# Moving the start of a background job inside one pair of a four-layer convolution kernel

## The chip, the cores and the metric

The kernel runs on one core of a Trainium2 chip, in one launch. The metric is the device time of that launch in microseconds (us); the time before is the median of three runs.

## What is computed

The input x has the shape 1024 x 16 x 16 x 16 (batch, height, width, channels), in float32. Four residual layers follow one another, each behind a group norm with 8 groups of 2 channels (mean and variance over height, width and the 2 channels of each sample):

```python
x = x + L0(gn(x))   # a tensor-train matrix on the 4096 values of a sample: cores of ranks 1, 16, 16, 1
x = x + L1(gn(x))   # a cellular automaton step: two depthwise 3x3 convolutions, 48 -> 128 -> 16 dense, an alive mask
x = x + L2(gn(x))   # a 3x3 convolution, 16 -> 16 channels
x = x + L3(gn(x))   # as L1, with other weights
```

The change lies in layer 0. What matters of the rest is that layer 1 needs the mean and the reciprocal root of the variance of layer 0's output, for each sample and group.

## The kernel before

**Halves and tiles.** The batch is cut in two halves of 512 samples. Two large SBUF tiles of 128 partitions x 32 x 512 floats, `XN[0]` and `XN[1]` (`xn` in the profile), hold activations. Layer 0 is done as 13 *pairs* (the rows of the table `OUTER`; `j` in the code, counted from 0). A pair multiplies combinations of input blocks by combinations of weight blocks. Pair j keeps its input in `XN[j % 2]`; the other large tile is being filled for pair j + 1.

**The foreground of a pair.** A pair has four *units* (u, by q from 0 to 3), and a unit has seven products (k from 0 to 6), each in two halves. So a pair has 4 x 7 x 2 = 56 *steps*, 14 to a unit; step 14 is the first of the second unit. A step issues eight matmuls (L1586). Around them, by the number of the step in its unit, stand: at 1 the store of the unit before (with one negated copy, L1553, and accumulating DMAs to `xf` on the queue of GpSimd, L1560); at 2, 4, 6, 12 and 13 a `mix` on VectorE, which makes the weights that a product needs from sums of blocks (L1508 and L1510): the ones at 12 and 13 (`s2`, `s5`) are for the next unit, whose first two products read them; at 5 and 9 a `build` of the next unit's weights, which is 32 small matmuls (L1478) and four copies on ScalarE (L1483); at 7 and 11 the loads for the unit after the next (`gq`; on GpSimd's queue at L1464 for pair 11, on SyncE's at L1459 for pair 12). After each second half a `gather` takes the product from PSUM: for the products 2, 3 and 6 in one VectorE addition of 128 x 1024 (L1622), for 4 and 5 in one of 128 x 512 (L1632), for 0 and 1 on ScalarE (L1628, L1630). In the first unit of a pair, ten additions on VectorE (L1220) also make the combined inputs of the pair.

**The order.** Every engine runs its instructions in the order in which the program issues them (`manual_schedule`, with all engines and SyncE's queue in order). The order is thus set by hand, by `run`: it goes through the 56 steps and, after each, issues background work that has fallen due. Background work comes as *spans*, `(list, lo, hi)`: the list is laid out between the fractions `lo` and `hi` of the pair. An entry of the list is a piece of work with a cost, or a bare number, which is a pause in us. Pauses are laid out as they are, by a nominal 107 us for a pair, but shrunk to 0.7 of the span if they would take more; the rest of the span is shared among the works by their costs. `run` waits for nothing: it only chooses the place in the order.

**The background of pair 11** has three spans:

- `part_steps(12)`, from 0.12 to 0.9: the input of pair 12. Four loads of 1 MB into `XN[0]` (L1249), four additions (L1259) from them, then eight pieces of 512 KB (`piece`, L1296) which are loaded two ahead of their use, each added by one VectorE addition (L1259). The pieces and the negated copies share four buffers.
- `ahead(...)` and `roots_ahead`, from 0.02 to 0.96, called *the statistics* below. This is a part of layer 1's group norm for the first half of the batch, done while layer 0 still works on the second half. It has two jobs, the last two of four variances (of the quarters 2 and 3). A job takes four loads of 512 KB from `xf` into six rotating slots in the upper part of `XN[0]` (L920, eight loads in both jobs, three ahead; and one mean from `means`, L924), for each a subtraction of the mean on VectorE (L936) and a square on ScalarE (L937); three additions into the job's first slot (L940) and a last one of half the width (L944); then a matmul (L957) and a short VectorE copy (L964). A slot can be loaded anew when its reader is done; load 6 of the eight goes into the slot that the first job sums into, and so waits for that job's L944. When both jobs are done, the root follows: a square root on ScalarE (L811), four Newton groups of five VectorE instructions (L818 to L822) on 128 columns each, then four times a matmul that spreads the result (L992), a copy on ScalarE (L996) and a DMA to `roots` (L997). The quarters 0 and 1 of the variances are made in pair 10.
- Four accumulating DMAs of the residual on GpSimd's queue (L1358), from 0.05 to 0.95.

Pair 12 reads `means` and `roots` back (L1011) from 0.15 of its length on, to normalise what will be layer 1's input (L1016).

Of the kernel before, what the change touches and what calls it, by code (L numbers as in the profile page):

```python
# [105 lines left out]
def conv_preact_kernel(ctx: ExitStack, tc: tile.TileContext, a: dict, out: bass.AP):  # L106
# [17 lines left out]
    def stage(es, sb, ps):  # L124

        for key, sizes, kw in (("sb", sb, {}), ("ps", ps, {"space": PSUM})):
            p = es.enter_context(
                tc.tile_pool(name=f"{key}{len(pool)}", bufs=1, reuse_waits="tile", **kw)
            )
            pool[key] = p, sizes  # L130
        pool[len(pool)] = None

    def work(shape, tag, name, dt=F32):
        p, sizes = pool["sb"]
        return p.tile(shape, dt, tag=tag, name=name, bufs=sizes[tag])
# [1057 lines left out]
    def first_normed(b, i):  # L1193

        X, E = part_tile(0)
        cols = slice(256 * i, 256 * i + 256)

        def op(t, k):
            x = X[:, b, t : t + 4, i]
            centre_scale(x, x if b else raw[:, t : t + 4, i], 0, cols, k)  # L1200

        return [(1.2, lambda t=t, k=k: op(t, k)) for t in (0, 4) for k in range(2)]

    def combined(p, ks=range(5)):


        X, E = part_tile(p)

        def op(t, k):
            h = slice(t, t + 4)  # L1210
            x = {(b, n): X[:, b, h, n] for b in range(2) for n in range(2)}
            e = [E[:, j, h] for j in range(3)]
            out, y, z, f = [
                (x[1, 0], x[1, 0], x[0, 0], ALU.subtract),
                (e[0], x[0, 0], x[1, 1], ALU.add),
                (e[1], x[1, 0], e[0], ALU.add),
                (e[2], x[0, 0], x[0, 1], ALU.add),
                (x[0, 1], x[0, 1], x[1, 1], ALU.subtract),
            ][k]
            V.tensor_tensor(out, y, z, f)  # L1220

        return [(1.2, lambda t=t, k=k: op(t, k)) for k in ks for t in (0, 4)]
# [783 lines left out]
    def run(layer, us, loads, *spans, by=0.0):  # L2006

        start, main = layer
        start()
        loads, done = list(loads), 0
        todo = []
        for bg, lo, hi in spans:
            bg = [b if isinstance(b, tuple) else (1, b) if callable(b) else (b, None) for b in bg]
            idle = sum(b[0] for b in bg if b[1] is None) / (us * (hi - lo))
            less = min(1.0, 0.7 / idle) if idle else 1.0
            weight = sum(b[0] for b in bg if b[1] is not None) or 1.0
            at = lo  # L2020
            for cost, step in bg:
                if step is None:
                    at += cost * less / us
                else:
                    todo.append((at, step))
                    at += (hi - lo) * (1 - idle * less) * cost / weight
        todo.sort(key=lambda x: x[0])
        for i, step in enumerate(main):
            step()
            part = (i + 1) / len(main)  # L2030
            while done < len(loads) and done < len(loads) * part / (by or 1e-9):
                loads[done]()
                done += 1
            while todo and (todo[0][0] < part or i == len(main) - 1):
                near = getattr(step, "dense", True) or i == len(main) - 1
                if getattr(todo[0][1], "beside", False) and not near:
                    break
                todo.pop(0)[1]()

    def put(L):  # L2040
        return lambda: nc.sync.dma_start(pack, L["pack"])
# [4 lines left out]
    def steps_of(*more):  # L2046
        return (lambda: None), [x for m in more for x in m]

    def now(steps):
        for step in steps:  # L2050
            step = step[1] if isinstance(step, tuple) else step
            if callable(step):
                step()
# [5 lines left out]
    with ExitStack() as es:  # L2059
        stage(es, dict(t4=4, s=2, n=2, w1=1, w0=2, s2=1, s5=1, r=1, gq=2, R=2, A=1), dict(w=4, m=1, o=3))  # L2060
        sums, cores, early, rest, sum_steps = train_setup(flats[0][:, 8192:9216])
        tag = ["w"]
        loads, stat, lines, tail, (spread0, spread1), kept = input_steps(0, tag, nc.sync)
        now(loads)

        A.activation(work([P, NB], "n", "warm")[:, 0:1], ident[:, 0:1], AF.Sqrt)
        (coefs, gload, build, mix), phases = layer_train()
        now([sums])
        coefs(0)
        now([cores] + stat[0])  # L2070
        early()
        gload(0, 1, queue=G)
        gload(0, 0, queue=G)
        now(lines[0])
        kept(0)
        kept(1)
        gload(1, 0)
        gload(1, 1)
        build(0, 1)
        build(0, 0)  # L2080
        now(stat[1] + tail[:2])
        mix(0, "s2")
        now([spread0] + tail[2:] + [spread1])
        x00, x11, x10, x01 = (first_normed(*at) for at in ((0, 0), (1, 1), (1, 0), (0, 1)))
        now(x00[0::2] + x00[1::2])
        mix(0, "s5")
        now(x11[:2])
        tag[0] = "m"
        more = combined(0)
        before = {  # L2090
            1: x11[2:] + rest[0][0:1],
            2: x10 + rest[0][1:2] + more[0:2],
            4: more[2:4],
            5: more[4:6],
            7: x01,
            8: more[6:8],
            9: more[8:10],
        }
        free = (12, 15, 18, 22, 26, 29, 32, 36, 40, 43)
        for i, piece in zip(free, rest[0][2:] + rest[1]):  # L2100
            before[i] = [piece]

        def woven_into(j, before):
            phases[j] = [
                lambda i=i, step=step: (now(before.get(i, ())), step()) for i, step in enumerate(phases[j])
            ]

        def sums_late(j):
            c = combined(j)
            woven_into(j, {2 * k + 1: c[2 * k : 2 * k + 2] for k in range(5)})  # L2110

        late = range(1, NP)
        woven_into(0, before)
        for j in late:
            sums_late(j)
        run(
            steps_of(phases[0]), 107, (), (lines[1], 0.12, 0.42), (part_steps(1), 0.43, 0.99),
        )
        tag.append("w")
        loads, stat, lines, tail, more, _ = input_steps(1, tag, G)  # L2120
        tail += [(0, more[0]), 2, (0, more[1]), 2]
        stat = [[stat[0][i] for i in range(4)], [(2.6, s1[1]) for s1 in stat[1][0::2]], stat[1][1::2]]
        woven_in = [x for i in range(4) for x in [stat[0][i]] + lines[0][4 * i : 4 * i + 4]]
        woven_in += [(0, loads[7])]
        for i in range(4):
            woven_in += [stat[1][i], stat[2][i]] + lines[1][4 * i : 4 * i + 4]
        run(
            steps_of(phases[1]), 107, (), ([(0, x) for x in loads[:7]] + [8] + woven_in + tail, 0.0, 0.76),
            (sum_steps(), 0.3, 0.55), (part_steps(2), 0.78, 1.0),
        )  # L2130
        root = {}
        aside = {
            2: (set1, 0.85),
            6: (fold1, 0.92),
            7: (set3, 0.75),
            8: (conv_weights(rooms[1]), 0.9),
            9: (fold3, 0.92),
            10: (ahead([(0, 0), (0, 1), (0, 2), (0, 3), (1, 0), (1, 1)], root, rooms[1]), 0.96),
            11: (ahead([(1, 2), (1, 3)], root, rooms[0]) + roots_ahead(root), 0.96),
        }  # L2140
        share = {2: 3, 4: 3, 5: 1, 6: 4, 7: 3, 8: 1, 9: 1, 10: 2, 11: 4}
        terms = residual_steps(0, range(16)) + residual_steps(1, range(16))
        for j in range(2, NP - 1):
            spans = [(part_steps(j + 1), 0.12, 0.9)]
            if j in aside:
                spans.append((aside[j][0], 0.02, aside[j][1]))
            n = share.get(j, 0)
            spans.append((terms[:n], 0.05, 0.95))
            del terms[:n]
            run(steps_of(phases[j]), 107, (), *spans)  # L2150
        fetches, parts = zip(*[applied(X0, q) for q in range(4)])
        bg = [fetches[0], 3]
        for q in range(4):
            bg += parts[q][:6] + list(fetches[q + 1 : q + 2]) + parts[q][6:]
        run(
            steps_of(phases[NP - 1]), 107, load_cw(X0, xf[0]) + [put(L1)], (bg, 0.15, 0.98),
            (terms, 0.05, 0.95), by=0.4,
        )
# [62 lines left out]
```

## Time and profile before

| | |
|---|---|
| median of 3 runs | 2737.14 us (2736.14 to 2738.66) |
| the profiled execution | 2737.21 us, its span 2734.2 us |
| granted TensorE clock, mean | 0.991 |
| busy: TensorE (PE), VectorE (DVE), ScalarE (ACT), GpSimd (POOL) | 98%, 73%, 45%, 20% |
| pairs 10, 11 and 12 begin at (first matmul of L1586) | 1207.9, 1327.7 and 1445.9 us |

The span is the time from the first instruction to the last one; the 3.0 us between it and the execution's own time lie around the program. In rows of instructions the columns are start, duration, engine, line, operation, output and inputs, shapes, and in brackets the idle time of the engine before it with what ended it. In rows of windows each engine has its busy time and its number of instructions, then follow the granted TensorE clock as a share of full speed, the busy share of the DMA engines and their rate (GB/s, which is kB per us). PEld is TensorE's weight load, SPq is SyncE's queue. The two DMA queues that carry data are called q1 (issued by SyncE) and q0 (issued by GpSimd).

### The profile page before, as it was taken

The numbers are of one execution on the slowest core, as the hardware profiler recorded it, in microseconds if no ns is written. First come the engines' busy times: TensorE is split into PE (matmuls) and PEld (weight loads), VectorE is DVE, ScalarE is ACT, GpSimd is POOL, SyncE is SP. The second block draws the span as 40 slices with busy tenths as digits, with TensorE's granted clock in tenths as the row PEclk, the third lists the DMA queues.
The fourth block names the chain that finished last, engine by engine and source line by source line (L and its number), as shares of the span: only waits on it lengthen the run. The fifth ranks groups of instructions, "written<-read, shape, count | busy, mean of one in ns | idle before, by whom it ended". The sixth has DMA issues, their size and how long they took to land.

```text
span 2734.2 us, 47225 instructions
## 1 busy us (share of the span) xinstructions
PE 2668.0 (98%) x18990; PEld 1749.5 (64%) x18990; DVE 1994.9 (73%) x2414; ACT 1241.6 (45%) x2091; POOL 542.9 (20%) x702
## 2 busy tenths in 40 slices
PE   6999999999999999999999999999999999999997
PEld 5888888888888888888878733433333333334344
DVE  8597667867788776667888677668779858756654
ACT  3324222222232222323322366676767757676664
POOL 2001351312122632311321111111113211110000
PEclk8999999999999999999999999999999999999998
DMA  6687788998797887888689664455576865444665
GB/s 255 214 317 271 228 173 220 240 202 199 188 250 182 156 216 186 205 237 250 178 188 259 138 170 101 107 161 121 107 195 84 202 155 139 99 89 118 179 176 209
DMA packets 265945, 503.19 MB, mean 184 GB/s; under 512 B 34404, under 2 KB 102040, under 8 KB 256448
## 3 DMA queue, kind: packets, MB, share of 16 engines
q1 hardware_dynamic: 179600, 336.68, 36.9%
q0 software_dynamic: 85936, 163.37, 34.0%
q8 instruction: 150, 2.46, 0.4%
q14 instruction: 67, 0.55, 0.1%
q10 hardware_dynamic: 192, 0.13, 0.0%
HBM read 281.71 MB, written 226.49 MB: 186 GB/s over the span
## 4 chain that ended last, share of the span: by engine, by line
PE 84%; DVE 7%; DMA 5%; issue 2%; ACT 1%; SPq 1%; POOL 0%; DVEq 0%; POOLq 0%; ACTq 0%
PE po L1586 40%; PE ph L1993 21%; PE po L1822 8%; PE po L1677 5%; PE pw L1478 4%; DMA xn<-in_x_dram 1%; DVE xn L1191 1%; PE po L1686 1%; DMA xn<-xr 1%; DMA g_sum<-g_dram 1%; DMA xn<-xf 1%; PE ptx L1886 1%; DVE xn L1220 1%; DMA xb<-xn 0%; PE pcnt L1862 0%
## 5 line engine op out<-in xcount | busy, mean ns | idle before, releaser
L1996 ACT ACTIVATE hid<-ph,pack 128x512 f32<-128x512 f32 (+1 forms) x1040 | 641.4, 684 | 313.5 <-PE ph L1993 254.6
L1586 PE MATMUL po<-xn,s 128*128 128x256 f32 x3328 | 756.0, 384 | 10.1 <-DVE s L1508 7.4
L1586 PEld LDWEIGHTS po<-xn,s 128*128 128x128 f32 x3328 | 628.5, 191 | 113.1 <-issue 16.1
L1586 PE MATMUL po<-xn,w 128*128 128x256 f32 x2496 | 565.2, 382 | 1.5 <-DVE xn L1220 1.5
L1993 PE MATMUL ph<-xn,wq 32*128 32x512 f32 (+1 forms) x3752 | 518.3, 590 | 1.9 <-DVE u L1834 1.5
L1586 PEld LDWEIGHTS po<-xn,w 128*128 128x128 f32 x2496 | 468.1, 190 | 74.6 <-issue 5.9
L1483 ACT COPY w<-pw 128x512 f32<-128x512 f32 x416 | 213.6, 599 | 455.6 <-PE pw L1478 379.9
L1993 PEld LDWEIGHTS ph<-xn,wq 32*128 32x128 f32 x3752 | 233.6, 184 | 228.9 <-issue 210.0
L1993 PE MATMUL ph<-xn,pack 32*128 32x512 f32 x1288 | 274.2, 607 | 5.6 <-DVE u L1834 1.6
L1508 DVE TENSOR_TENSOR s<-w 128x1024 f32<-128x1024 f32 x208 | 251.3, 1218 | 29.0 <-PE po L1586 25.9
L1822 PE MATMUL po<-hid,pack 128*32 128x512 f32 (+1 forms) x2080 | 256.0, 592 | 0.8 <-ACT hid L1996 0.5
L1834 DVE SCALAR_TENSOR_TENSOR u<-po,pack,xn 128x512 f32<-128x512 f32 (+1 forms) x130 | 96.3, 741 | 168.1 <-PE po L1822 167.0
L1876 POOL DMA_DIRECT2D xf<-u x96 | 82.6, 861 | 618.7 <-DVE u L1874 591.0
L771 DVE TENSOR_TENSOR xn<-xn,m 128x1024 f32<-128x1024 f32 x128 | 150.2, 1217 | 34.7 <-ACT m L794 34.6
L1993 PEld LDWEIGHTS ph<-xn,pack 32*128 32x128 f32 x1288 | 115.6, 184 | 90.8 <-issue 63.2
L1822 PEld LDWEIGHTS po<-hid,pack 128*32 128x32 f32 x2080 | 53.9, 109 | 174.9 <-ACT hid L1996 86.3
L1677 PE MATMUL po<-xn,convw 128*128 128x512 f32 x368 | 163.6, 598 | 0.0
L1220 DVE TENSOR_TENSOR xn<-xn 128x1024 f32<-128x1024 f32 x130 | 152.6, 1215 | 0.0
L1478 PE MATMUL pw<-R,gq 32*128 32x128 f32 x3328 | 139.4, 286 | 7.9 <-DVE small L1133 7.3
L1622 DVE TENSOR_TENSOR r<-r,po 128x1024 f32<-128x1024 f32 x78 | 95.0, 1218 | 70.5 <-PE po L1586 57.5
L1478 PEld LDWEIGHTS pw<-R,gq 32*128 32x128 f32 x3328 | 113.9, 188 | 42.2 <-issue 38.6
L1560 POOL DMA_DIRECT2D xf<-xn x69 | 88.6, 1733 | 254.2 <-DVE xn L1553 72.3
(230 smaller groups left out, 2764.7 us busy)
## 6 DMA issues: line engine op xcount, KB each, us to landing
xn<-xf SPq DMA_DIRECT2D x128, 512.0 KB
xn<-xb SPq DMA_DIRECT2D x36, 1024.0 KB
wq<-L_conv_wy SPq DMA_DIRECT2D x192, 192.0 KB
xf<-xn POOLq DMA_DIRECT2D x69, 512.0 KB, 9.7
piece<-xb SPq DMA_DIRECT2D x64, 512.0 KB
xf<-r POOLq DMA_DIRECT2D x48, 512.0 KB, 11.7
xf<-u POOLq DMA_DIRECT2D x96, 256.0 KB, 4.1
gq<-g_dram SPq DMA_DIRECT2D x86, 256.0 KB
```

Of the source, the lines that this page charges most:

```text
L771: V.tensor_tensor(part, part, m().unsqueeze(1).broadcast_to([P, 2, NB]), op)
L1220: V.tensor_tensor(out, y, z, f)
L1478: T.matmul(pw[r][:, v, i], g[rows, P * (2 * v + i) : P * (2 * v + i) + P], R[rows, k], start=k == 0, stop=k == len(gs) - 1,)
L1483: A.copy(w.rearrange("p b s t m -> p (b s t) m")[:, :, 32 * r : 32 * r + 32].rearrange("p k (v o) -> p v k o", v=2), pw[r].rearrange("p v ...
L1508: V.tensor_tensor(t.rearrange("p s t m -> p (s t m)"), x, y, f)
L1586: T.matmul(po[:, i], matrix(u, what)[:, i, t], x, start=t == 0, stop=t == 3)
L1622: V.tensor_tensor(part, part, po.unsqueeze(2).broadcast_to([P, 2, 2, 256]), ALU.add)
L1677: T.matmul(st["po", h][wh], conv["fw"][:, y], X[:, 16 * wh + h + y - 1], start=y == max(0, 1 - h), stop=y == min(2, S - h),)
L1822: T.matmul(po[32 * j : 32 * j + 32], nca["w1"][:, v], hid[j], start=v == 0, stop=v == 1)
L1834: V.scalar_tensor_tensor(u, po, nca["b1"], X[:, 8 * q + w2, cols(hf)], ALU.add, ALU.add)
L1993: T.matmul(ph, w, x, start=k == 0, stop=k == len(tiles) - 1)
L1996: A.activation(h, ph, AF.Relu, bias=nca["bt"][:, r : r + 1])
```

## The change

The span of the statistics starts at 0.2 of pair 11 in place of 0.02. Its end stays at 0.96, and so does all that is computed; pairs 2 to 10 keep their spans.

```diff
         for j in range(2, NP - 1):
             spans = [(part_steps(j + 1), 0.12, 0.9)]
             if j in aside:
-                spans.append((aside[j][0], 0.02, aside[j][1]))
+                spans.append((aside[j][0], 0.2 if j == 11 else 0.02, aside[j][1]))
             n = share.get(j, 0)
             spans.append((terms[:n], 0.05, 0.95))
             del terms[:n]
             run(steps_of(phases[j]), 107, (), *spans)
```

## The prediction

> **What bounds the kernel now.** I read the page first: engines, then the chain that ended last.
>
> ```profile
> PE 2668.0 (98%) x18990; PEld 1749.5 (64%) x18990; DVE 1994.9 (73%) x2414; ACT 1241.6 (45%) x2091; POOL 542.9 (20%) x702
> ...
> PE po L1586 40%; PE ph L1993 21%; PE po L1822 8%; PE po L1677 5%; PE pw L1478 4%; DMA xn<-in_x_dram 1%; DVE xn L1191 1%; PE po L1686 1%; DMA xn<-xr 1%; DMA g_sum<-g_dram 1%; DMA xn<-xf 1%; PE ptx L1886 1%; DVE xn L1220 1%; DMA xb<-xn 0%; PE pcnt L1862 0%
> ```
>
> TensorE is almost never idle, and layer 0's products (L1586) are the longest part. The statistics run on other engines, so the change can only remove or create TensorE waits. Next, busy time by window: units 0 and 1 of pair 11, and unit 0 of pair 12.
>
> ```profile
> 1327.70:1357.00 29.30, 26.93 (x178) 22.91 (x176) 28.15 (x27) 9.34 (x15) 11.18 (x19) 1.00 0.86 263
> 1357.00:1386.60 29.60, 29.60 (x179) 24.27 (x180) 28.02 (x27) 11.45 (x17) 8.18 (x12) 0.95 0.74 187
> ...
> 1445.90:1472.70 26.80, 26.80 (x178) 23.09 (x177) 24.50 (x23) 6.28 (x12) 6.40 (x6) 1.00 1.06 297
> ```
>
> A unit with nothing extra on TensorE takes 26.8 us. Unit 0 of pair 11 has 2.5 us more, with VectorE (third engine) busy 28.15 of 29.30. Unit 1 has 2.8 more, of which one variance matmul pair (L957) is 1.2 (unit 3, with three pairs of that size, takes 30.3, so 3.5/3 each); the other 1.6 goes with a clock of 0.95. The waits of TensorE in pair 11 are a single one. The timeline around it:
>
> ```profile
> 1354.48 1.22 DVE L940 TENSOR_TENSOR xn<-xn 128x1024 f32<-128x1024 f32 x1
> 1355.62 1.22 DVE L1508 TENSOR_TENSOR s<-w 128x1024 f32<-128x1024 f32 x1
> ...
> 1356.98 5.24 PE L1586 MATMUL po<-xn,s 128*128 128x256 f32 x16 [2.37 <-DVE s L1508]
> ```
>
> Unit 1's first product needs `s2` (L1508), which stood behind the statistics (L936, L940) in VectorE's queue. Windows on L1586 show the aftermath:
>
> ```profile
> 1349.60:1353.00 3.40, 3.40 (x18) 2.99 (x17) 1.00 0.40 107
> 1356.70:1360.10 3.40, 3.12 (x8) 2.52 (x8) 0.50 0.08 24
> ```
>
> After the 2.37 us wait the clock was 0.50 for 3.4 us, with 8 matmuls in place of 18: that is the 1.6 us. A shorter wait in pair 3 kept the clock at 1.00:
>
> ```profile
> 477.62 4.55 PE L1586 MATMUL po<-xn,s 128*128 128x256 f32 x20 [1.31 <-DVE s L1508]
> ```
>
> **Where the pieces go.** A unit is 14 steps and two builds of 1.17 (row of L1478), so a step is (26.8 - 2.34)/14 = 1.75 us. The statistics' list has works of cost 31.4 and pauses of 63.6. Before, the span is 0.94 of the nominal 107 us; pauses take 0.63 of it, and a Newton group (cost 1.7) spans (0.94 x 0.37 x 1.7/31.4) x 56 = 1.05 steps. After, pauses would be 63.6/(0.76 x 107) = 0.78 of the span and are capped at 0.7, so a Newton group spans 0.76 x 0.3 x 1.7/31.4 x 56 = 0.69 step. Walking the list, the places (step after which it is issued, before -> after) are: first three loads 1 -> 11; first L936 5 -> 14; first job's L944 14 -> 22; load 6 15 -> 22; square root 31 -> 35; Newton groups 33, 35, 36, 37 -> 37, 38, 38, 39; spreads 41, 44, 47, 50 -> 43, 45, 48, 51. The pieces stay: pieces 0 and 1 are fetched after step 22, piece 0 added after 24, pieces 3, 4 and 5 after 34, 37 and 40. The places before match the order of VectorE's rows.
>
> **Removed: the wait at step 14.** Three L936 and two L940 leave VectorE's queue ahead of `s2`: 5 x 1.135 (spacing of such rows) = 5.7 us, and an idle 1.12 of the first L940. Then `s2` waits only for the gather of step 11, whose product is ready at 1327.7 + 23.3 = 1351.0. With 0.6 and 1.22 it is done by 1352.9, and TensorE wants it at 1354.45. The whole wait and its slow clock go: **-2.5 - 1.6 = -4.1 us**.
>
> **Added: a wait at step 28.** TensorE gets there at 1354.45 + 26.8 + 1.2 (L957) = 1382.4. VectorE has, from 1354.45 to the first job's L944, three gathers, three L1259, one negation, three mixes, four L936 and three L940: 17 x 1.135 + 0.6 = 19.9, to 1374.4. SyncE's queue stands behind that L944: load 6 needs its slot, and piece 0 is issued after load 6. Before, load 6 went out 19 us before piece 0 was used. SyncE's rows and windows of the transfers:
>
> ```profile
> 1363.26 0.87 SPq L920 DMA_DIRECT2D xn<-xf  x2
> 1364.19 12.43 SPq L1296 DMA_DIRECT2D piece<-xb  x4
> ```
> ```profile
> 1366.00:1367.00 1.00, 1.00 (x6) 0.90 (x5) 1.00 (x2) 1.00 (x3) 1.00 (x2) 1.00 1.07 414
> ...
> 1369.00:1370.00 1.00, 1.00 (x7) 0.80 (x5) 1.00 (x1) 1.00 (x1) 0.00 (x0) 1.00 0.80 213
> ```
>
> A load's 524 kB passed by 1366.4, 3.1 us after issue (63 + 311 kB by 1366.0, the rest at 414). A piece's 524 kB at 213 take 2.45. From the last byte to VectorE's start, the loads issued at 1243.83 give 0.85: the first load's bytes end at 1248.75 by the rates, and the row waiting for it starts at 1249.61.
>
> ```profile
> 1249.61 1.23 DVE L940 TENSOR_TENSOR xn<-xn 128x1024 f32<-128x1024 f32 x1 [3.04 <-DMA xn<-xf]
> ```
>
> So piece 0 can be added at 1374.4 + 3.1 + 2.45 + 0.85 = 1380.8. Behind that addition on VectorE stand the gather of step 25 (0.6), L964 (0.7) and `s2` (1.22): done at 1384.5. The wait is 2.1 us, bounds 0 (landing by 1378.7) and 4.4: the load at 1243.83 began to move at 1247, 3.2 after issue where the one at 1363.26 took 0.9, because q0 was busy. I take the quiet row: moved 4 us forward, unit 0's store and residual on q0 should end near 1374. Slow clock after it: 0 (the 1.31 row) to 1.6; I take 1.6, as 2.1 is nearer to 2.37. **+3.7 us**.
>
> **Added: a wait at step 42.** Newton groups as VectorE shows them:
>
> ```profile
> 1399.48 0.94 DVE L818 RECIPROCAL r<-t 128x128 f32<-128x128 f32 x1
> ...
> 1401.58 1.22 DVE L1510 TENSOR_TENSOR w<-w 128x1024 f32<-128x1024 f32 x1
> ...
> 1409.19 0.68 DVE L1632 TENSOR_TENSOR xn<-xn,po 128x512 f32<-128x512 f32 x1
> ...
> 1413.62 1.22 DVE L1508 TENSOR_TENSOR s<-w 128x1024 f32<-128x1024 f32 x1
> ```
>
> A group takes 2.1 us. Before, one group stood between the gather of step 37 (1409.19) and unit 3's `s2` (1413.62). After, all four do: gather 0.6, a piece's addition 1.135, groups 6.3, gather 0.6, group 2.1, `s2` 1.22, in all 11.95. TensorE, from that gather's product to step 42, has one build and four steps: 1.17 + 7.0 = 8.15. The wait is 3.8 us. VectorE can't begin earlier, since the gather comes first in its order. Bounds: 2.6 if TensorE is held by 1.2 in between (before, one spread stood after step 41), 4.5 if the piece lands late. Slow clock 1.6. **+5.4 us**.
>
> [...]
>
> **Costed at nothing.** The first three loads leave a quiet stretch (1313 to 1322) and join pair 12's loads; their first use is now near 1356.7, over 10 us after those, and pair 12's loads wait for TensorE (to 1326), not for them. The `gq` loads behind the residual on q0 landed at 1353.7 for a build at 1365: if q0 slows by 5 us, nothing is late. Square root, spreads and stores of roots hang on VectorE's result only; the last spread and copy come after step 51 (50 and 51 before), and pair 12 reads from its step 8 on. TensorE bounds what follows, so a shift passes on.
>
> **Sum**: -4.1 + 3.7 + 5.4 = +5.0 us. On the span 2734.2 + 5.0 = 2739.2; the profiled run's own time, 2737.21, is 0.07 above the median, so the median becomes 2737.14 + 5.0 = **2742.1**. About 0.2% (5.5 us, so 2742.6) is what a measurement of this kernel can tell from no change; the forecast lies just below that.
>
> **Rivals.**
> - *The transfer starts late.* q0 is still busy at 1374, and load 6 has the 3.2 us start: the wait at 28 is 4.4 and slow clock is sure, +7.3, 2744.4. For: three stores and a residual (2 MB) on q0. Against: they are issued 4 us earlier.
> - *Piece 0 is in time.* No wait at 28: -4.1 + 5.4 = +1.3, 2738.4. Against: it needs landing 2.1 us sooner than both rows give.
> - *Faster: Newton work lies earlier.* If two of the four groups come before the gather of step 37, where VectorE has idle time, 4.2 us leave the 11.95 and step 42 has no wait. With piece 0 landing by 1378.7 only the gain is left: -4.1, 2733.0. It decides at 3.8 us of Newton work ahead of that gather. Against: the places worked out, and the square root waiting for L964 after step 34.
> - *Nothing.* Another work takes the removed places and the same wait stays: 2737.1. Against: the wait ended on VectorE alone, with 6.8 us of statistics before it.
>
> **Chances.** Forecast (both waits, quiet start) 0.50, its own range 2740.5 (clock kept at 28) to 2743.5 (piece 0.7 later, 0.7 more at 42), of which I put 0.25 above 2742.6; late transfer 0.28; piece in time 0.10; faster 0.08; nothing 0.04. Faster 0.08, within 0.2% 0.39, slower 0.53. The range 2738.4 to 2746.0 leaves out the last two rivals and the late transfer's upper end.
>
> **What would show it.** Right: no wait at step 14, TensorE waits on L1508 near 1382 and 1412 of about 2 and 4 us, each with a stretch of clock 0.50, L1259 waiting for `piece` near 1378. Wrong: a single wait, or DVE idle between 1404 and 1413.

## The result

The change makes the kernel slower by a little: 2743.77 us median of 15 runs after it, against 2737.64 us median of 15 runs before it. The ratio is 1.0021, with a 95% interval from 1.0014 to 1.0028. By the ratio that is 5.7 us, between 3.8 and 7.7 (the two medians lie 6.1 us apart). The profiled execution after the change took 2741.47 us, with a span of 2739.8 us, 5.6 more than the span before.

**The profile after the change.** The windows of the four units of pair 11 and of the first unit of pair 12 (columns as before: window, length, PE, PEld, DVE, ACT, POOL with instructions, clock, DMA share, GB/s):

```profile
1327.80:1354.50 26.70, 26.70 (x177) 23.03 (x176) 23.47 (x22) 6.28 (x12) 8.76 (x14) 1.00 1.05 322
1354.50:1385.40 30.90, 28.14 (x179) 22.97 (x179) 27.06 (x26) 12.07 (x18) 15.80 (x27) 1.00 0.87 206
1385.40:1418.00 32.60, 28.09 (x179) 23.18 (x179) 31.32 (x43) 8.80 (x15) 4.61 (x4) 1.00 0.79 183
1418.00:1451.10 33.10, 33.10 (x184) 25.16 (x185) 17.21 (x18) 8.46 (x16) 3.64 (x3) 0.95 0.47 108
1451.10:1477.90 26.80, 26.80 (x178) 23.09 (x177) 24.47 (x23) 6.28 (x12) 6.41 (x6) 1.00 1.07 295
```

Unit 0 has become a plain unit of 26.7 us: the wait at step 14 is gone. Units 1 and 2 now lose time to idle TensorE (PE busy is 2.8 and 4.5 us under the length), and unit 3 has the lower clock, 0.95. Pair 11 takes 123.3 us (1327.8 to 1451.1) where it took 118.2. So 5.1 of the 5.6 us of the span lie in this pair. What TensorE waits for in it (in total, times, longest):

```profile
PE po L1586 <- DVE s L1508: 6.7, 2, 3.9
PE pvar L957 <- DVE s1s L944: 0.6, 1, 0.6
```

One wait has become two, both on VectorE's weights (`s`), and a small one at the second variance matmul. VectorE before the first of them:

```profile
1374.39 0.69 DVE L944 TENSOR_TENSOR s1s<-xn 128x512 f32<-128x512 f32 x1
1375.00 1.22 DVE L936 TENSOR_TENSOR xn<-xn,xn 128x1024 f32<-128x1024 f32 x1
1376.14 0.68 DVE L1632 TENSOR_TENSOR r<-r,po 128x512 f32<-128x512 f32 x1
1376.74 1.22 DVE L936 TENSOR_TENSOR xn<-xn,xn 128x1024 f32<-128x1024 f32 x1
1381.46 1.22 DVE L1259 TENSOR_TENSOR xn<-xn,piece 128x1024 f32<-128x1024 f32 x1 [3.51 <-DMA piece<-xb]
...
1384.04 1.23 DVE L1508 TENSOR_TENSOR s<-w 128x1024 f32<-128x1024 f32 x1
```

VectorE idles 3.51 us for piece 0, with `s2` behind it. SyncE's queue shows why the piece came late: load 6 (L920) left at 1375.11, as soon as the first job's L944 had ended (1375.08), and piece 0 right after it.

```profile
1375.11 0.36 SPq L920 DMA_DIRECT2D xn<-xf  x1
1375.52 0.95 SPq L1296 DMA_DIRECT2D piece<-xb  x2
```

TensorE's side of both waits, and the Newton groups ahead of the second one (each group begins with L818; the rows of L819 to L822 between them are left out):

```profile
1385.41 7.14 PE L1586 MATMUL po<-xn,s 128*128 128x256 f32 x32 [2.77 <-DVE s L1508]
...
1417.97 2.59 PE L1586 MATMUL po<-xn,s 128*128 128x256 f32 x7 [3.94 <-DVE s L1508]
```
```profile
1405.86 0.69 DVE L1632 TENSOR_TENSOR xn<-xn,po 128x512 f32<-128x512 f32 x1 [0.59 <-PE po L1586]
...
1407.60 0.95 DVE L818 RECIPROCAL r<-t 128x128 f32<-128x128 f32 x1
...
1414.50 0.94 DVE L818 RECIPROCAL r<-t 128x128 f32<-128x128 f32 x1
...
1416.60 1.22 DVE L1508 TENSOR_TENSOR s<-w 128x1024 f32<-128x1024 f32 x1
```

From the gather of step 37 to the end of `s2` VectorE is busy for 11.96 us without a pause (1405.86 to 1417.82). All four groups stand in between. The windows of L1586 after each wait (PE, PEld, clock, DMA share, GB/s):

```profile
1385.40:1388.80 3.40, 3.39 (x16) 3.01 (x17) 1.00 1.08 298
1418.70:1422.10 3.40, 3.40 (x10) 2.69 (x9) 0.50 0.02 5
```

After 2.77 us of idling the clock stayed at full speed; after 3.94 us it was 0.50 for 3.4 us (the last section sets the waits side by side).

### The profile page after: what moved, and what is told of

The parts are those of the page before. It is cut to its first block, busy times and chain, and to the rows that moved or that the text cites. A ratio compares the mean times of both kernels' runs of the same rounds, so it can differ in the third digit from the quotient of the medians.

```text
span 2739.8 us, 47224 instructions
## 1 busy us (share of the span) xinstructions
PE 2666.1 (97%) x18990; PEld 1747.8 (64%) x18990; DVE 1995.1 (73%) x2414; ACT 1241.0 (45%) x2091; POOL 541.2 (20%) x702
## 4 chain that ended last, share of the span: by engine, by line
PE 83%; DVE 8%; DMA 5%; issue 2%; ACT 1%; SPq 1%; POOL 0%; DVEq 0%; POOLq 0%; ACTq 0%
PE po L1586 40%; PE ph L1993 21%; PE po L1822 8%; PE po L1677 5%; PE pw L1478 4%; DMA xn<-in_x_dram 1%; DVE xn L1191 1%; PE po L1686 1%; DMA xn<-xr 1%; DMA g_sum<-g_dram 1%; DMA xn<-xf 1%; PE ptx L1886 1%; DVE s L1508 1%; DMA xb<-xn 0%; DVE u L1834 0%
## 5 line engine op out<-in xcount | busy, mean ns | idle before, releaser
L1586 PE MATMUL po<-xn,s 128*128 128x256 f32 x3328 | 753.6, 383 | 14.5 <-DVE s L1508 11.9
L1586 PEld LDWEIGHTS po<-xn,s 128*128 128x128 f32 x3328 | 627.8, 191 | 115.6 <-issue 20.5
L1586 PE MATMUL po<-xn,w 128*128 128x256 f32 x2496 | 567.1, 382 | 2.5 <-DVE xn L1220 2.5
L1586 PEld LDWEIGHTS po<-xn,w 128*128 128x128 f32 x2496 | 469.1, 190 | 77.8 <-issue 7.4
L1508 DVE TENSOR_TENSOR s<-w 128x1024 f32<-128x1024 f32 x208 | 251.3, 1218 | 29.9 <-PE po L1586 26.6
```

The lines of the kernel that those rows point to most:

```text
L1508: V.tensor_tensor(t.rearrange("p s t m -> p (s t m)"), x, y, f)
L1586: T.matmul(po[:, i], matrix(u, what)[:, i, t], x, start=t == 0, stop=t == 3)
```

## The experiments

The theory: a wait at step 28 that comes from SyncE's order (piece 0 behind load 6, load 6 behind L944), and a wait at step 42 that comes from four Newton groups ahead of `s2`. Two rivals: that the three loads which the change moves onto pair 12's loads slow the transfers, and that VectorE simply has more work than it can do in the shorter stretch, so that a wait taken away at one place comes back at the next. In all of them but the plain repeat, a helper lays the list of the statistics out by `run`'s own formula and then moves single entries; the diffs shown are excerpts, with comments added, and `at[k][0]` is the place of an entry as a fraction of the pair, so that (s + 0.5)/56 is the place after step s.

**Pieces 0 and 1 ahead of load 6** (`e2_pieces_first`), otherwise the changed kernel:

```diff
+            if j == 11:
+                at = laid(spans.pop()[0], 0.12, 0.9)
+                at[8][0] = at[9][0] = 17.5 / 56     # the fetches of pieces 0 and 1
+                spans = [([x], t, t + 0.001) for t, x in at]
```

> The changed kernel, but the loads of pieces 0 and 1 are issued after step 17, ahead of load 6 in SyncE's queue. My theory: piece 0 is there long before its addition, so VectorE does not idle near 1378 and the wait at step 28 (2.8 us) and the short wait of the second variance matmul (0.6) go; the wait at step 42 stays at 3.9 with its slow clock. Pair 11 takes about 123.3 - 3.4 = 119.9 us. Rival, contention of the three moved loads on the transfers: the pieces and the loads compete as before, and the wait at 28 stays above 1.5 us.

Its pieces left SyncE's queue early, and VectorE did not idle for piece 0 (it added it at 1379.91, directly behind the row before):

```profile
1339.31 6.84 SPq L1296 DMA_DIRECT2D piece<-xb  x2
1346.20 31.83 SPq L920 DMA_DIRECT2D xn<-xf  x4
```
```profile
PE po L1586 <- DVE s L1508: 3.9, 1, 3.9
PE pvar L957 <- DVE s1s L944: 0.2, 1, 0.2
```

The wait at step 28 is gone, the one at 42 is what it was. Pair 11 took 120.0 us (1329.8 to 1449.8). The ratio to the kernel before was 1.0005 (0.9996 to 1.0014). The order in one queue was the cause; the three moved loads stood where the change puts them, so contention from them would have left the wait.

**The moved loads at their old place** (`e4_loads_early`), otherwise the changed kernel:

```diff
+                for k, (t, _) in enumerate(laid(aside[j][0], 0.02, aside[j][1])[:4]):
+                    at[k][0] = t     # the first mean and loads 0 to 2, after step 1
```

> The changed kernel, but the first mean and the first three loads of the statistics are issued after step 1, as before the change; all other work has the places of the changed kernel. My theory: their place costs nothing, both waits stay (about 2.8 and 3.9 us), and pair 11 takes 123.3 us within 1 us, or 1.6 more if the clock drops after step 28. Rival, contention: taking the three loads off the stretch of pair 12's loads lets pieces and queue q0 run ahead, and the wait at step 28 falls by over 1.5 us.

The waits were 2.29 and 3.93 us, and pair 11 took 124.8 us (1331.2 to 1456.0); ratio 1.0020 (1.0011 to 1.0029). The wait at 28 fell by 0.5 us, not by the 1.5 of the rival; as it was 2.61 to 2.79 us in the four traces with moved loads and late pieces (the changed kernel twice, `e1_newton_late`, `e7_newton_split`), up to half a microsecond may be due to the place of the loads. Here the clock did drop after it:

```profile
1388.40 3.81 PE L1586 MATMUL po<-xn,s 128*128 128x256 f32 x11 [2.29 <-DVE s L1508]
```
```profile
1389.70:1393.10 3.40, 3.40 (x10) 2.69 (x9) 0.50 0.87 268
```

That pair 11 is 1.5 us longer here than in the changed kernel is a matter of the clock. The drop costs 1.7 us (32 matmuls took 8.67 us in place of 6.98) and hides the wait of 0.6 us at the second variance matmul, and after the wait of 3.93 us the clock was 0.50 for 6.8 us in place of 3.4, from 1420.39 to 1427.22.

**Three Newton groups behind the weights, first try** (`e1_newton_late`; and `e3_both`, which has the edit of the pieces as well):

```diff
+                for k, step in zip(range(-11, 0), (41, 43, 44, 46, 47, 48, 49, 50, 51, 52, 53)):
+                    at[k][0] = (step + 0.5) / 56   # Newton 1, 2, 3, then spread, copy, spread, copy ...
```

> The changed kernel, but the last three Newton groups are issued after steps 41, 43 and 44, behind unit 3's weights s2 and s5, and the spreads and copies after steps 46 to 53. My theory: the wait at step 42 is the Newton groups ahead of s2, so it goes with its slow clock (3.9 + 1.8 us), and the wait at step 28 (2.8) stays. Pair 11 takes 123.3 - 5.7 = 117.6 us, about 0.6 less than before the change; 1.6 more if the clock drops after step 28. Rival, a backlog of VectorE as a whole: the wait only moves to the next weights (the start of pair 12), and pair 11 and 12 together gain under 2 us. Rival, contention of the three moved loads: no change, 123.3.

> The changed kernel with both edits: pieces 0 and 1 fetched after step 17, three Newton groups and the spreads later. My theory: no wait on L1508 is left in pair 11, and it takes four plain units and six small matmul pairs, 4 x 26.8 + 6 x 1.15 = 114.1 us, 4.1 less than before the change (time ratio to before 0.9985). Rival, a backlog of VectorE as a whole: a wait of 2 us or more is left at some later weights, and pair 11 with pair 12 is not under the time before by more than 2 us.

Both expectations were missed. Pair 11 took 126.1 us in the first kernel (1331.1 to 1457.2) and 121.7 in the second (1329.7 to 1451.4); the ratios were 1.0028 (1.0017 to 1.0040) and 1.0014 (1.0005 to 1.0022). The waits of TensorE in `e3_both` from unit 2 to the start of pair 12:

```profile
PE pr L992 <- DVE r L822: 3.9, 1, 3.9
PE pr L992 <- ACT m L996: 1.4, 2, 0.7
PE pvar L957 <- DVE s1s L944: 0.2, 1, 0.2
```

There is no wait on L1508 any more, as the theory has it. But a new wait of the same size stands at the first spread (L992; 3.9 us in `e1_newton_late` too, beside the 2.8 of step 28): it was issued after step 46, and TensorE, whose matmuls keep the order of issue here, stood before it until VectorE had done Newton group 3 at 1425.1. The next spreads waited for ScalarE's copies of the ones before. So these kernels show the edit's own fault more than they test the rival, and the edit was made again.

**Two Newton groups behind the weights, spreads late enough** (`e7_newton_split`; and `e6_both_again` with the edit of the pieces):

```diff
+                for k, step in zip(range(-10, 0), (41, 41, 46, 46, 48, 48, 50, 50, 52, 52)):
+                    at[k][0] = (step + 0.5) / 56   # Newton 2 and 3, then each spread with its copy
```

> The changed kernel with only the second of these edits: Newton groups 2 and 3 after step 41, spreads and copies after 46, 48, 50, 52; pieces are fetched as in the changed kernel. My theory: the wait at step 28 (2.5 to 2.9 us, plus 1.6 where the clock drops) is the only one left, with 0.6 at the second variance matmul: pair 11 takes 117.6 to 119.2 us, within 1 us of the time before. Rival, backlog: the wait at step 28 pushes VectorE so far back that a wait of over 2 us comes again at step 42.

> The changed kernel with pieces 0 and 1 fetched after step 17 and two Newton groups moved: groups 0 and 1 keep their places (after 37 and 38), groups 2 and 3 come after step 41, behind s2 and s5, and each spread with its copy after steps 46, 48, 50 and 52, late enough for VectorE to be done. My theory: between the gather of step 37 and s2 stand 0.6 + 1.14 + 4.2 + 0.6 + 1.22 = 7.8 us in the 8.15 that TensorE takes, so no wait is left at 14, 28, 42 or before a spread: pair 11 takes 114.1 us, 4.1 less than before the change and 9 less than the changed kernel. Rival, a backlog of VectorE as a whole: 2 us or more of waits are left somewhere in pair 11 or 12.

In `e7_newton_split` pair 11 took 117.7 us (1329.3 to 1447.0) and the ratio was 1.0000 (0.9991 to 1.0009). The waits left were those of step 28 and the variance matmul:

```profile
PE po L1586 <- DVE s L1508: 2.6, 1, 2.6
PE pvar L957 <- DVE s1s L944: 0.6, 1, 0.6
```

In `e6_both_again` no wait on the weights or before a spread is left. Its windows of units 0 to 3:

```profile
1329.40:1356.10 26.70, 26.70 (x177) 23.03 (x176) 23.49 (x22) 6.28 (x12) 8.52 (x14) 1.00 1.05 324
1356.10:1384.10 28.00, 28.00 (x180) 23.16 (x180) 27.52 (x26) 12.06 (x18) 16.03 (x27) 1.00 0.96 237
1384.10:1412.10 28.00, 27.81 (x179) 23.15 (x178) 26.97 (x34) 8.80 (x15) 4.61 (x4) 1.00 0.87 201
1412.10:1443.90 31.80, 31.80 (x186) 23.95 (x186) 20.83 (x28) 8.62 (x16) 3.64 (x3) 1.00 0.50 115
```

Pair 11 took 114.5 us (1329.4 to 1443.9), with the clock at 1.00 throughout, and the kernel is a little faster even than the one before the change: 2735.46 us against 2738.48, ratio 0.9988 (0.9979 to 0.9997). The rival of a general backlog falls with it: the same statistics in the same shortened stretch leave no wait but 0.2 us at the variance matmul, once three places in the order are changed.

**The Newton places alone, in the kernel before** (`e5_newton_only`): the statistics begin at 0.02, and only the groups, spreads and copies have the places of the changed kernel.

```diff
+                at = laid(aside[j][0], 0.02, aside[j][1])
+                moved = laid(aside[j][0], 0.2, aside[j][1])
+                for k in range(-12, 0):
+                    at[k][0] = moved[k][0]
```

> The kernel before the change (statistics from 0.02), with only the Newton groups, spreads and copies at the places of the changed kernel: groups after steps 37, 38, 38 and 39. My theory: the order of the Newton groups alone makes the wait at step 42. Pair 11 keeps the wait at step 14 (2.4 us, slow clock 1.6) and gets one of 3.9 with 1.7 at step 42: 118.2 + 5.6 = 123.8 us, total 5 to 6 us over the time before. Rival, the backlog of VectorE from the denser jobs makes it: the jobs stand here as before, so the wait at step 42 stays under 1.5 us.

```profile
PE po L1586 <- DVE s L1508: 6.3, 2, 3.9
```

The two waits are the old one at step 14 (2.38 us) and 3.94 us at step 42, each followed by slow matmuls of L1586 (6 in 2.70 us and 9 in 3.81, where 16 take 3.62 at full clock); pair 11 took 124.2 us (1330.4 to 1454.6) and the ratio was 1.0017 (1.0008 to 1.0026). The jobs stood as before the change, so the order of the Newton groups makes the wait at step 42 by itself.

**The changed kernel again** (`r1_after_again`, one run for its profile):

> The changed kernel once more, unaltered, for its profile. My theory: the waits at steps 28 and 42 come again at 2.8 and 3.9 us within 0.5, since they follow from the order alone; whether the clock drops after the first is left open by the rows so far (dropped after a wait of 2.37, not after one of 2.77), and pair 11 takes 123.3 us, or 124.9 with a drop.

Pair 11 took 123.3 us again (1327.5 to 1450.8), with waits of 6.7 us on L1508, the longest 3.9, and so no drop of the clock after the first, which would have made it 124.9.

## Why the prediction was right

**The removed wait** was sized well. Unit 0 went from 29.3 to 26.7 us, and the slow clock that had followed in unit 1 is gone: 2.5 + 1.6 us, as worked out. The added waits take back what was gained here and more.

**The wait at step 28** came at the place and by the chain that were foreseen: L944 at 1374.39 (its end counted as 1374.4 in the sum, in fact 1375.08), load 6, piece 0, `s2`. From load 6's issue to piece 0's addition passed 6.35 us, where the rows of before gave 3.1 + 2.45 + 0.85 = 6.4. That the total agrees so closely is luck: by the bytes that q1 moved, load 6's 524 kB took 3.5 us from their issue, piece 0's 1.7, and 1.2 passed from there to the addition. The whole wait was 2.8 in place of 2.1, and the 0.7 is L944 ending later. The quiet start was the right choice: q0's large transfers had ended by 1374.5 (from 1374 to 1376 the DMA engines were 16% busy), and load 6 began to move 1.05 us after its issue. The prediction's 0.9 for the load at 1363.26 was too short, though: its first bytes moved 1.3 us after its issue, and those of the load at 1243.83 after 3.3.

**The slow clock after it** was the term that was off: 1.6 in the sum, 0 in both profiles of the changed kernel. The prediction chose by the length of the wait, and the length alone does not tell: 2.77 us kept the clock here, 2.76 us in pair 1 of the kernel before lost it (last section). The sum was saved, by luck, by two smaller misses the other way: the 0.7 above, and a wait of 0.6 at the second variance matmul that was not seen, since the second job's L944 is pushed back by the same idle time of VectorE (with the pieces early it is 0.2).

**The wait at step 42** was 3.94, worked out as 3.8 (11.95 us of VectorE's work against 8.15 of TensorE's), and the slow clock behind it 1.7 (unit 3 took 33.1, plain 31.4), worked out as 1.6. `e5_newton_only` and `e7_newton_split` show that nothing else is needed for it. By one of its own signs the prediction would count as wrong, VectorE idling between 1404 and 1413: it did, for 0.59 us before the gather of step 37 at 1405.86. But that lies ahead of the work that the sum counts, and takes nothing from it.

**The sum** by the trace is -2.5 - 1.6 + 2.8 + 0.6 + 3.9 + 1.7 = +4.9, and the pair grew by 5.1; the prediction had +5.0. The measured 5.7 us (3.8 to 7.7) agree. The waits and their places are thus right by their mechanism, the closeness of the total partly by chance. That the timed runs lie a little above the profiled ones would fit a drop of the clock after step 28 in some of them, as in `e4_loads_early`; there are no traces of them, so this stays open. The moved loads, put at nothing, may have cost up to the 0.5 us of `e4_loads_early`.

**The rivals.** The late transfer did not happen. Piece 0 was not in time. The faster outcome needed Newton work ahead of the gather of step 37, and there was none; but its price was right: with the waits at 28 and 42 taken away, `e6_both_again` gains 3.7 us in pair 11 of the 4.1 worked out.

## What to carry to other kernels

Shifting a background job to where an engine has room also shifts every entry behind it and packs them closer: look for the critical instruction that each entry now stands in front of, on its own engine and on the DMA queue, since a load that waits there for a freed buffer holds back the prefetch behind it, as load 6 did with piece 0 (VectorE idle for 3.51 us). Sum the work between the instruction that releases an engine and the one that another engine needs, and compare it with the time that the other engine takes; here that gave each wait to within 0.7 us. And when such work is moved behind the critical instruction, move its consumers as well, or the wait goes with it, as the first two trials showed.

## What was not expected of the hardware

The length of a short wait does not tell, in these traces, whether TensorE's clock drops. Waits of 2.29 (`e4_loads_early`) and 2.37 us (before) were followed by 3.4 us at 0.50, and one of 2.38 us (`e5_newton_only`) by 6 matmuls in 2.70 us, where 16 take 3.62 us at full clock. After the wait of 2.77 us in the changed kernel the clock stayed at 1.00, and by the length of pair 11 it stayed after 2.8 us in the repeat (123.3 us again) and after 2.6 us in `e7_newton_split` (117.7 us, 3.2 over the 114.5 of `e6_both_again`, of which the longer waits are 3.0). But waits of 2.76 (before) and 2.98 us (the changed kernel) at the start of pair 1 lost the clock: 3.4 us at 0.50 in both, and 32 matmuls in 8.83 us, where the 32 behind the wait of 2.77 us took 7.14. In pair 3, where these kernels issue the same instructions, waits of 1.31 (before) and 1.52 us (the changed kernel) kept it and one of 2.15 lost it (`e5_newton_only`: 24 matmuls in 7.11 us, which take 5.45 at full clock).

What decides between a drop and none, no run here was made to show. The price of a drop was 1.6 us (step 14 before) to 1.7 us (step 42 after, and 8.83 - 7.14 in pair 1), or some 2.5 us in `e4_loads_early`, where the half clock lasted 6.8 us. On these rows, a wait of 2.1 to 3 us is thus to be counted with a range for the clock, from nothing to 1.7 us. The waits of 3.9 us in pair 11 lost it in the changed kernel (0.50 for 3.4 us), in `e4_loads_early` and `e5_newton_only`, and in `e3_both` (8 matmuls in 3.42 us behind the first spread, 1.99 at full clock). The wait at step 14 lost it in both traces that have it (2.37 and 2.38 us).
